# A graph network in fp32 on one core: the product h by seven half-size products with partial sums read from the banks, and first loads in blocks on two queues

## The chip, the cores and the metric

The kernel runs on one core of a Trainium2 chip. The metric is the device time of one execution in microseconds (us). Executions of one kernel mostly agree within 0.3%, so a difference of a few us is judged by several runs of both kernels in turn on the same chip.

PE is TensorE's matmul, PEld its weight load, DVE VectorE, ACT ScalarE, POOL GpSimd, SP SyncE; SPq, ACTq and POOLq are those engines issuing transfers.

## The reference

There are 4096 nodes with 512 features, all in fp32.

```python
# layer 0
bw = sign(w0); ba = max(sign(x), 0)
x = layernorm(x + relu(adj @ (ba @ bw.T)))
# layer 1
node_att = softmax(x @ node_w, axis=0)
h = x @ edge_w                                  # 4096 x 512: the change makes this cheaper
e = where(adj > 0, h @ h.T, -9e15)              # 4096 x 4096 scores
combined = node_att * softmax(e, axis=1)
x = layernorm(x + (adj * combined) @ (x @ w1) + bias)
```

## The kernel before

Four stages fill the time: x@w of layer 0 (bf16 signs), the aggregation over adj, h, and the scores h @ h.T in pairs of 512x512 blocks. The last stage, the weighted sum, runs on seven half-size products already (`lop` and `q` below), as did the preparation of its left operands.

```python
# start: one load for each of w0 and x^T, signed whole
w0 = stream.tile([P, KD, D], F32, name="w0", tag="stream")
nc.sync.dma_start(w0, w0_t.rearrange("(k p) o -> p k o", p=P))
# ... neg and bw on VectorE; nw_b, bias_b and we_s (1 MB) loaded by GpSimd
for g in range(NG):                                   # 8 groups of 512 rows
    xt = stream.tile([P, KD, W], F32, name="xt", tag="stream")
    nc.sync.dma_start(xt, x_t[:, ts(g, W)].rearrange("(k p) n -> p k n", p=P))
    ba = sp.tile([P, KD, W], BF16, name="ba", tag="hi")
    nc.vector.tensor_scalar(ba, xt, 0.0, None, ALU.is_gt)
    for j in range(BG):
        pw = ps_mm.tile([P, D], F32, name="pw", tag="mm")
        for k in range(KD):
            nc.tensor.matmul(pw, ba[:, k, ts(j, P)], bw[:, k, :], start=(k == 0), stop=(k == KD - 1))
        nc.scalar.copy(xw[:, g * BG + j, :], pw)

def aggregate(b):                                     # one of 32 row blocks of adj @ xw
    xb = rows.tile([P, D], F32, name="xb", tag="rows")
    nc.gpsimd.dma_start(xb, x[ts(b, P), :])           # 256 KB, on the GpSimd queue
    # ... 64 matmuls into acc, layernorm into xb, node_s and x1_d from it

for g in range(NG):                                   # h, transposed, over x1T in place
    ph = []
    for m in range(KD):
        p = ps_mm.tile([P, W], F32, name="ph", tag="mm")
        for k in range(KD):
            nc.tensor.matmul(p, we_s[:, k, ts(m, P)], x1T[:, k, ts(g, W)], start=(k == 0), stop=(k == KD - 1))
        ph.append(p)
    # ... copies of ph into x1T on ScalarE and VectorE
hT = x1T

blk = ctx.enter_context(tc.tile_pool(name="blk", bufs=11))    # takes the place that xw had
lopp = ctx.enter_context(tc.tile_pool(name="lopp", bufs=4))
adjp = ctx.enter_context(tc.tile_pool(name="adjp", bufs=2))

class Scores:                                          # one pair (A, B) of 512-row groups
    def load(self):                                    # 1 MB of adj for each direction
        a = blk.tile([P, BG, W], F32, name="a", tag="blk")
        nc.sync.dma_start(a, adj[ts(r, W), ts(c, W)].rearrange("(b p) w -> p b w", p=P))
    # prepare: one VectorE op on each a; main: scores pe, ScalarE's copy s, stats of them on VectorE;
    # turn: PE transposes s into pt; end: s and its transpose are stored to HBM

class Aggregate:                                       # the weighted sum, after all scores
    def load(self):
        a = adjp.tile([P, BG, BG, P], F32, name="ac")  # 1 MB of adj^T
        nc.gpsimd.dma_start(a, adj_t[ts(c, BG), :, ts(r, BG), :].rearrange("b p c i -> p b c i"))
    def main(self, between):
        lop = lopp.tile([P, BG, HD], F32, name="lop")  # 0.5 MB
        nc.sync.dma_start(lop, lop_d[self.r][:, m])
```

The point to keep in mind: the first two `ac` and four `lop` loads have free buffers, so they are issued as soon as h allows, although nothing uses them until about 1137 us. They share the transfer engines with the `a` blocks that the scores need at once.

Of the kernel before, what the change touches and what calls it, by code (L numbers as in the profile page):

```python
# [11 lines left out]
F32 = mybir.dt.float32  # L12
BF16 = mybir.dt.bfloat16
F32R = mybir.dt.float32r
AF = mybir.ActivationFunctionType
ALU = mybir.AluOpType
AX = mybir.AxisListType

P = 128
EPS = 1e-5  # L20
NEG_BIG = -9000000000000000.0
HUGE = 3.4e38


@with_exitstack
def kernel(
# [13 lines left out]
    nc = tc.nc  # L40
    N, D = x.shape
    NB = N // P
# [29 lines left out]
    lop_d = [dram.tile([P, 7, BG, HD], F32, name=f"lop_d{g}") for g in range(HG)]  # L72


    x1T = big.tile([P, KD, N], F32, name="x1T", tag="feat_major")

    def layernorm(ts_):
        n = len(ts_)
# [11 lines left out]
    with (  # L90
        tc.tile_pool(name="wide", bufs=1) as wide,
        tc.tile_pool(name="stream", bufs=3) as stream,
        tc.tile_pool(name="weights", bufs=1) as wp,
        tc.tile_pool(name="signs", bufs=2) as sp,
    ):

        xw = wide.tile([P, NB, D], F32R, name="xw", tag="node_major")
        nw_b = wp.tile([P, D], F32, name="nw_b")
        nc.gpsimd.dma_start(nw_b, bass.AP(tensor=node_w.tensor, offset=node_w.offset, ap=[[0, P], [1, D]]))

        bias_b = wp.tile([P, D], F32, name="bias_b")
        nc.gpsimd.dma_start(bias_b, bass.AP(tensor=bias.tensor, offset=bias.offset, ap=[[0, P], [1, D]]))


        w0 = stream.tile([P, KD, D], F32, name="w0", tag="stream")
        nc.sync.dma_start(w0, w0_t.rearrange("(k p) o -> p k o", p=P))
        neg = sp.tile([P, KD, D], BF16, name="neg", tag="hi")
        nc.vector.tensor_scalar(neg, w0, 0.0, None, ALU.is_lt)
        bw = wp.tile([P, KD, D], BF16, name="bw")
        nc.vector.scalar_tensor_tensor(bw, w0, 0.0, neg, ALU.is_gt, ALU.subtract)  # L110

        we_s = wp.tile([P, KD, D], F32, name="we_s")
        nc.gpsimd.dma_start(we_s, edge_w.rearrange("(k p) o -> p k o", p=P))

        for g in range(NG):
            xt = stream.tile([P, KD, W], F32, name="xt", tag="stream")
            nc.sync.dma_start(xt, x_t[:, ts(g, W)].rearrange("(k p) n -> p k n", p=P))
            ba = sp.tile([P, KD, W], BF16, name="ba", tag="hi")
            nc.vector.tensor_scalar(ba, xt, 0.0, None, ALU.is_gt)
            for j in range(BG):  # L120
                pw = ps_mm.tile([P, D], F32, name="pw", tag="mm")
                for k in range(KD):
                    nc.tensor.matmul(pw, ba[:, k, ts(j, P)], bw[:, k, :], start=(k == 0), stop=(k == KD - 1))  # L123
                nc.scalar.copy(xw[:, g * BG + j, :], pw)


        def aggregate(b):
            xb = rows.tile([P, D], F32, name="xb", tag="rows")
            nc.gpsimd.dma_start(xb, x[ts(b, P), :])
            acc = ps_mm.tile([P, D], F32, name="acc", tag="mm")  # L130
            for half in range(2):
                at = stream.tile([P, HB, P], F32, name="at", tag="stream")
                nc.sync.dma_start(at, adj_t[b, :, ts(half, HB), :])

                for q in range(2):
                    aq = at[:, ts(q, QC), :]
                    hi = sp.tile([P, QC, P], F32R, name="hi", tag="hi")
                    nc.scalar.copy(hi, aq)  # L138
                    lo = sp.tile([P, QC, P], F32R, name="lo", tag="lo")
                    nc.vector.tensor_sub(lo, aq, hi.bitcast(F32))  # L140
                    for c in range(QC):
                        kb = half * HB + q * QC + c
                        nc.tensor.matmul(acc, hi[:, c, :], xw[:, kb, :], start=(kb == 0), stop=False)  # L143
                        nc.tensor.matmul(acc, lo[:, c, :], xw[:, kb, :], start=False, stop=(kb == NB - 1))  # L144
            nc.vector.scalar_tensor_tensor(xb, acc, 0.0, xb, ALU.max, ALU.add)
            layernorm([xb])
            scr = wp.tile([P, D], F32, name="scr")
            nc.vector.tensor_tensor_reduce(
                scr, xb, nw_b, 1.0, 0.0, ALU.mult, ALU.add, accum_out=node_s[:, b : b + 1]
            )  # L150
            nc.gpsimd.tensor_add(scr, xb, bias_b)
            nc.gpsimd.dma_start(x1_d[ts(b, P), :], scr)
            return xb

        def left(b, low, high):

            to = lop_d[b // BG][:, :, b % BG, :]
            l11, l21, l12, l22 = low[:, :HD], low[:, HD:], high[:, :HD], high[:, HD:]
            sums_l = wp.tile([P, 4, HD], F32, name="sums_l", bufs=2)
            s4, s1, s2, s3 = (sums_l[:, n, :] for n in range(4))  # L160
            nc.gpsimd.tensor_sub(s3, l11, l21)
            nc.gpsimd.tensor_add(s1, l22, l21)
            nc.gpsimd.tensor_sub(s2, s1, l11)
            nc.gpsimd.tensor_sub(s4, l12, s2)
            nc.gpsimd.dma_start(to[:, 0, :], l11)
            nc.gpsimd.dma_start(to[:, 1:4:2, :], high.rearrange("p (h f) -> p h f", h=2))
            nc.gpsimd.dma_start(to[:, 2, :], s4)
            nc.gpsimd.dma_start(to[:, 4:, :], sums_l[:, 1:, :])

        def transpose_rows(b, xb):  # L170
            pt = ps_tr.tile([P, KD, P], F32, name="pt", tag="tr")
            for k in range(KD):
                nc.tensor.transpose(pt[:, k, :], xb[:, ts(k, P)], ident)  # L173
            nc.scalar.copy(x1T[:, :, ts(b, P)], pt)

        before = None
        for n in range(NB):
            b = n // 2 + n % 2 * HB
            xb = aggregate(b)
            if n % 2:  # L180
                left(n // 2, before[1], xb)
            if before is not None:
                transpose_rows(*before)
            before = (b, xb)
        transpose_rows(*before)


        for g in range(NG):
            ph = []
            for m in range(KD):  # L190
                p = ps_mm.tile([P, W], F32, name="ph", tag="mm")
                for k in range(KD):
                    nc.tensor.matmul(p, we_s[:, k, ts(m, P)], x1T[:, k, ts(g, W)], start=(k == 0), stop=(k == KD - 1))  # L193
                ph.append(p)
            for m in range(KD):
                if m % 2:
                    nc.vector.tensor_copy(x1T[:, m, ts(g, W)], ph[m])
                else:
                    nc.scalar.copy(x1T[:, m, ts(g, W)], ph[m])
    hT = x1T  # L200


    nmax = const.tile([P, 1], F32, name="nmax")
# [281 lines left out]
        some(1)  # L485


    over = big.tile([P, KD * N], F32, name="over", tag="feat_major")
    sums = over[:, : 2 * 7 * 2 * W].rearrange("p (g m h w) -> p g m h w", g=2, m=7, h=2)
    w1_s = over[:, 2 * 7 * 2 * W :].rearrange("p (k o) -> p k o", o=D)  # L490
    nc.sync.dma_start(w1_s, w1.rearrange("(k p) o -> p k o", p=P))
# [66 lines left out]
```

## Time and profile before

| | us |
|---|---|
| median of the timed runs | 2053.45 (2051.93 to 2053.71) |
| span of the profiled run | 2048.1 |
| idle time of PE | 35 |
| of which at the start | 16.4 |
| of which just after h | 4.8 |

The lines that carry this stand in the prediction. A timeline line gives the start, the duration, the engine, the line of the kernel, the operation with output and input, the number of records, and in brackets the idle time before it with what ended it. A row of the stage table gives the stretch, then busy time (and instructions) of PE, PEld, DVE, ACT and POOL, then the granted clock, the share of the transfer engines that was busy, and GB/s. What stands ahead of the `a` blocks in the queues after h is not shown there, so here it is, from the timeline of the kernel before:

```profile
636.33 1.30 SPq L393 DMA_DIRECT2D lop<-lop_d  x3
...
636.56 1.71 POOL L343 DMA_DIRECT2D ac<-in_adj_t_dram  x2 [90.33 <-PE ph L193]
...
639.10 2.06 SPq L393 DMA_DIRECT2D lop<-lop_d  x1
```

Two MB of `lop` and two of `ac` are issued within 5 us of h's end at 636.10, most of them ahead of the sixth `a` block.

### The profile page before, as it was taken

The numbers are of one execution on the slowest core, as the hardware profiler recorded it, in microseconds if no ns is written. First come the engines' busy times: TensorE is split into PE (matmuls) and PEld (weight loads), VectorE is DVE, ScalarE is ACT, GpSimd is POOL, SyncE is SP. The second block draws the span as 40 slices with busy tenths as digits, with TensorE's granted clock in tenths as the row PEclk, the third lists the DMA queues.
The fourth block names the chain that finished last, engine by engine and source line by source line (L and its number), as shares of the span: only waits on it lengthen the run. The fifth ranks groups of instructions, "written<-read, shape, count | busy, mean of one in ns | idle before, by whom it ended". The sixth has DMA issues, their size and how long they took to land.

```text
span 2048.1 us, 17627 instructions
## 1 busy us (share of the span) xinstructions
PE 2013.1 (98%) x6288; PEld 1113.3 (54%) x6288; DVE 1213.0 (59%) x1713; ACT 692.3 (34%) x1195; POOL 407.3 (20%) x512
## 2 busy tenths in 40 slices
PE   6999999999999999999999999999999999999997
PEld 3888888888544455555455544444444444444443
DVE  3555555555312454445445898687759775977634
ACT  4333333333102666666666631121211310221100
POOL 0334343343200000000001111240114111321101
PEclk9999999999999999999999999999999999999999
DMA  8565665565304777768776987576757765675421
GB/s 303 192 206 199 211 216 194 199 218 180 131 0 185 259 277 256 279 223 307 259 254 240 356 312 278 202 274 228 265 200 272 258 243 194 249 262 204 174 78 61
DMA packets 115623, 455.71 MB, mean 223 GB/s; under 512 B 10192, under 2 KB 10192, under 8 KB 90960
## 3 DMA queue, kind: packets, MB, share of 16 engines
q0 software_dynamic: 51120, 251.16, 32.7%
q1 hardware_dynamic: 64416, 203.44, 30.0%
q8 instruction: 49, 0.80, 0.2%
q14 instruction: 38, 0.31, 0.0%
HBM read 355.99 MB, written 98.57 MB: 222 GB/s over the span
## 4 chain that ended last, share of the span: by engine, by line
PE 97%; DMA 2%; DVE 1%; issue 0%; ACT 0%; SPq 0%; POOLq 0%; POOL 0%; DVEq 0%
PE ps L397 38%; PE pe L274 21%; PE acc L144 11%; PE acc L143 11%; PE ph L193 5%; PE po L449 5%; PE pt L295 3%; PE pw L123 1%; DMA xt<-in_x_t_dram 1%; DMA a<-in_adj_dram 1%; PE pt L173 1%; PE ptm L323 0%; DMA xb<-x_d 0%; DVE lo L140 0%; DMA out_dram<-xb 0%
## 5 line engine op out<-in xcount | busy, mean ns | idle before, releaser
L274 PE MATMUL pe<-x1T 128*128 128x512 f32 (+3 forms) x1152 | 477.3, 558 | 0.0
L397 PE MATMUL ps<-q,lop 128*128 128x512 f32 x1024 | 446.9, 592 | 0.0
L143 PE MATMUL acc<-xw,hi 128*128 128x512 f32 x1024 | 401.6, 392 | 0.0
L144 PE MATMUL acc<-xw,lo 128*128 128x512 f32 x1024 | 399.2, 390 | 0.5 <-DVE lo L140 0.5
L397 PE MATMUL ps<-t,lop 128*128 128x512 f32 x768 | 332.9, 592 | 0.0
L397 PEld LDWEIGHTS ps<-q,lop 128*128 128x128 f32 x1024 | 193.9, 190 | 240.8 <-issue 237.2
L274 PEld LDWEIGHTS pe<-x1T 128*128 128x128 f32 x1152 | 205.7, 191 | 184.8 <-issue 175.9
L352 ACT ACTIVATE q<-q 128x2048 f32<-128x2048 f32 x64 | 122.3, 1911 | 412.3 <-DVE q L349 400.9
L140 DVE TENSOR_TENSOR lo<-at,hi 128x1024 fp32r<-128x1024 f32 x128 | 166.6, 1302 | 147.0 <-ACT hi L138 146.9
L397 PEld LDWEIGHTS ps<-t,lop 128*128 128x128 f32 x768 | 145.9, 190 | 183.7 <-issue 178.9
L138 ACT CAST hi<-at 128x1024 fp32r<-128x1024 f32 x128 | 134.6, 1051 | 272.5 <-PE acc L143 268.3
L358 DVE SCALAR_TENSOR_TENSOR q<-ac,q 128x512 f32<-128x512 f32 x256 | 195.2, 815 | 51.5 <-ACT q L352 37.6
L144 PEld LDWEIGHTS acc<-xw,lo 128*128 128x128 f32 x1024 | 192.3, 188 | 40.3 <-DVE lo L140 0.9
L143 PEld LDWEIGHTS acc<-xw,hi 128*128 128x128 f32 x1024 | 192.3, 188 | 39.3
L256 DVE CUSTOM_DVE_ANT_0 a<-a,pe 128x512 f32<-128x512 f32 x112 | 76.9, 687 | 215.1 <-ACT s L281 215.1
L260 ACT ACTIVATE a<-a,nmax_c 128x512 f32<-128x512 f32 x256 | 183.4, 718 | 47.8 <-DVE nmax_c L256 47.3
L349 DVE CUSTOM_DVE_ANT_1 q<-q,mrow 128x2048 f32<-128x2048 f32 x64 | 152.4, 2387 | 47.3 <-DMA q<-s_d 39.2
L401 DVE TENSOR_TENSOR over<-over,ps 128x512 f32<-128x512 f32 x168 | 113.6, 681 | 103.3 <-PE ps L397 103.2
L343 POOL DMA_DIRECT2D ac<-in_adj_t_dram x64 | 49.0, 765 | 387.7 <-DVE q L358 280.1
L281 ACT COPY s<-pe 128x512 f32<-128x512 f32 (+2 forms) x144 | 78.0, 544 | 138.4 <-PE pe L274 117.2
L449 PE MATMUL po<-over 128*128 128x512 f32 x256 | 114.2, 592 | 3.8 <-DVE xb L458 3.8
L193 PE MATMUL ph<-x1T,we_s 128*128 128x512 f32 x256 | 110.2, 592 | 0.0
(88 smaller groups left out, 1491.7 us busy)
## 6 DMA issues: line engine op xcount, KB each, us to landing
at<-in_adj_t_dram SPq DMA_DIRECT2D x64, 1024.0 KB, 5.0
a<-in_adj_dram SPq DMA_DIRECT2D x64, 1024.0 KB, 7.8
ac<-in_adj_t_dram POOLq DMA_DIRECT2D x64, 1024.0 KB, 6.9
q<-s_d POOLq DMA_DIRECT2D x64, 1024.0 KB, 8.1
lop<-lop_d SPq DMA_DIRECT2D x112, 512.0 KB, 4.3
s_d<-s POOLq DMA_DIRECT2D x36, 1024.0 KB, 4.8
s_d<-t POOLq DMA_DIRECT2D x28, 1024.0 KB, 7.0
xt<-in_x_t_dram SPq DMA_DIRECT2D x8, 1024.0 KB, 8.2
```

Source lines behind the costliest of these rows:

```text
L138: nc.scalar.copy(hi, aq)
L140: nc.vector.tensor_sub(lo, aq, hi.bitcast(F32))
L143: nc.tensor.matmul(acc, hi[:, c, :], xw[:, kb, :], start=(kb == 0), stop=False)
L144: nc.tensor.matmul(acc, lo[:, c, :], xw[:, kb, :], start=False, stop=(kb == NB - 1))
L193: nc.tensor.matmul(p, we_s[:, k, ts(m, P)], x1T[:, k, ts(g, W)], start=(k == 0), stop=(k == KD - 1))
L260: lambda: nc.scalar.activation(e, e, AF.Exp, bias=nmax_c[:, b, c : c + 1], scale=-1.0, accum_out=sum_c[:, b, c : c + 1])
L274: nc.tensor.matmul(pe[:, lo * P :], hT[:, k, ts(A * BG + i, P)], hT[:, k, (B * BG + lo) * P : (B + 1) * W], start=(k == 0), stop=(k == KD ...
L349: nc.vector._custom_dve(TENSOR_ADD_SAT, out=q, in0=q, in1=mrow.unsqueeze(1).to_broadcast([P, BG, W]), s0=0.0, s1=-HUGE)
L352: nc.scalar.activation(q, q, AF.Exp)
L358: nc.vector.scalar_tensor_tensor(qc, a[:, :, c, :], 0.0, qc, ALU.max, ALU.mult)
L397: nc.tensor.matmul(ps, lop[:, c, ts(h, P)], rop[m][:, c, :], start=(c == 0), stop=(c == BG - 1))
L449: nc.tensor.matmul(po, (lower if k // 2 else upper)[:, k % 2, ts(i, P)], w1_s[:, k, :], start=(k == 0), stop=(k == KD - 1),)
```

## The change

Its intent: h by seven products of half size in place of eight, which saves an eighth of its matmuls. Partial sums stay in the banks, are read there in mid-group, and are added onto. This needs x1T and the result hT in different places, so xw and x1T exchange theirs. The start brings w0 and the first x^T in four blocks each, from two queues, signs them by blocks, and runs 12 matmuls on zeros to warm the clock. `xb`, `bias`, `node_w` and `edge_w` (1 MB, now loaded during the aggregation) move to the SP queue.

```diff
-    x1T = big.tile([P, KD, N], F32, name="x1T", tag="feat_major")
+    xw = big.tile([P, NB, D], F32R, name="xw", tag="large")
+    def seven(lop, rop, dests, after):
+        banks = [[ps_mm.tile([P, W], F32, name="seven", tag="mm") for q in range(2)] for _ in range(3)]
+        def multiply(bank, m, first, then):
+            for q in range(2):
+                for k in range(K):
+                    nc.tensor.matmul(banks[bank][q], lop(m, q)[k], rop(m)[k],
+                        start=(first and k == 0), stop=(k == K - 1), skip_group_check=not first)
+                then(banks[bank][q], q, *dests[q])
...
+        multiply(0, 0, True, m1)
+        multiply(1, 5, True, u2)
+        multiply(2, 4, True, nothing)
+        multiply(1, 6, False, u3)
+        multiply(0, 1, False, m2)
+        multiply(1, 3, False, m4)
+        multiply(2, 2, False, m3)
...
+            if g == 0:
+                for k in range(KD):
+                    nc.sync.dma_start(w0[:, k, :], w0_t[ts(k, P), :])
+                    nc.scalar.dma_start(xt[:, k, :], x_t[ts(k, P), ts(g, W)])
+                for _ in range(WARM):
+                    nc.tensor.matmul(pws[0], warm[:, :P], warm, start=True, stop=True)
+                # signs by blocks of 128x512 on VectorE
...
-            nc.gpsimd.dma_start(xb, x[ts(b, P), :])
+            nc.sync.dma_start(xb, x[ts(b, P), :])
...
+        hT = big.tile([P, KD, N], F32, name="hT", tag="large")
+        for g in range(HG):
+            # t1..t4 from x1T: three subtractions on VectorE, one on GpSimd
+            seven(...)
```

More of the change, by code (lines that the diff above doesn't have):

```diff
@@ L22 @@
 HUGE = 3.4e38
+WARM = 12
 @with_exitstack
@@ L72, with m1, u2, nothing @@
     lop_d = [dram.tile([P, 7, BG, HD], F32, name=f"lop_d{g}") for g in range(HG)]
-    x1T = big.tile([P, KD, N], F32, name="x1T", tag="feat_major")
+    xw = big.tile([P, NB, D], F32R, name="xw", tag="large")
+    def seven(lop, rop, dests, after):
+        K = len(rop(0))
+        banks = [[ps_mm.tile([P, W], F32, name="seven", tag="mm") for q in range(2)] for _ in range(3)]
+        def multiply(bank, m, first, then):
+            for q in range(2):
+                for k in range(K):
+                    nc.tensor.matmul(
+                        banks[bank][q],
+                        lop(m, q)[k],
+                        rop(m)[k],
+                        start=(first and k == 0),
+                        stop=(k == K - 1),
+                        skip_group_check=not first,
+                    )
+                then(banks[bank][q], q, *dests[q])
+                after(None, None)
+        def m1(ps, q, c11, c12, c21, c22):
+            nc.scalar.copy(c21, ps)
+        def u2(ps, q, c11, c12, c21, c22):
+            nc.vector.tensor_add(c12, c21, ps)
+        def nothing(*_):
+            pass
+        def u3(ps, q, c11, c12, c21, c22):
+            nc.vector.tensor_add(c22, c21, ps)
+            nc.vector.tensor_add(c22, c22, banks[2][q])
+            after(q, 3)
+        def m2(ps, q, c11, c12, c21, c22):
+            nc.scalar.copy(c11, ps)
+            after(q, 0)
+        def m4(ps, q, c11, c12, c21, c22):
+            nc.vector.tensor_add(c21, c21, ps)
+            after(q, 2)
+        def m3(ps, q, c11, c12, c21, c22):
+            nc.vector.tensor_add(c12, c12, ps)
+            after(q, 1)
+        multiply(0, 0, True, m1)
[5 more added lines that the diff above has]
+        multiply(2, 2, False, m3)
     def layernorm(ts_):
@@ L95 @@
     ):
-        xw = wide.tile([P, NB, D], F32R, name="xw", tag="node_major")
-        nw_b = wp.tile([P, D], F32, name="nw_b")
-        nc.gpsimd.dma_start(nw_b, bass.AP(tensor=node_w.tensor, offset=node_w.offset, ap=[[0, P], [1, D]]))
-        bias_b = wp.tile([P, D], F32, name="bias_b")
-        nc.gpsimd.dma_start(bias_b, bass.AP(tensor=bias.tensor, offset=bias.offset, ap=[[0, P], [1, D]]))
+        x1T = wide.tile([P, KD, N], F32, name="x1T")
+        warm = wp.tile([P, W], BF16, name="warm")
@@ L105 @@
+        nc.vector.memset(warm, 0.0)
         w0 = stream.tile([P, KD, D], F32, name="w0", tag="stream")
-        nc.sync.dma_start(w0, w0_t.rearrange("(k p) o -> p k o", p=P))
-        neg = sp.tile([P, KD, D], BF16, name="neg", tag="hi")
-        nc.vector.tensor_scalar(neg, w0, 0.0, None, ALU.is_lt)
         bw = wp.tile([P, KD, D], BF16, name="bw")
-        nc.vector.scalar_tensor_tensor(bw, w0, 0.0, neg, ALU.is_gt, ALU.subtract)
-        we_s = wp.tile([P, KD, D], F32, name="we_s")
-        nc.gpsimd.dma_start(we_s, edge_w.rearrange("(k p) o -> p k o", p=P))
@@ L115 @@
         for g in range(NG):
             xt = stream.tile([P, KD, W], F32, name="xt", tag="stream")
-            nc.sync.dma_start(xt, x_t[:, ts(g, W)].rearrange("(k p) n -> p k n", p=P))
             ba = sp.tile([P, KD, W], BF16, name="ba", tag="hi")
-            nc.vector.tensor_scalar(ba, xt, 0.0, None, ALU.is_gt)
-            for j in range(BG):
-                pw = ps_mm.tile([P, D], F32, name="pw", tag="mm")
+            pws = [ps_mm.tile([P, D], F32, name="pw", tag="mm") for j in range(BG)]
@@ L122 @@
+            if g == 0:
+                neg = sp.tile([P, KD, D], BF16, name="neg", tag="lo")
                 for k in range(KD):
-                    nc.tensor.matmul(pw, ba[:, k, ts(j, P)], bw[:, k, :], start=(k == 0), stop=(k == KD - 1))
-                nc.scalar.copy(xw[:, g * BG + j, :], pw)
+                    nc.sync.dma_start(w0[:, k, :], w0_t[ts(k, P), :])
[3 more added lines that the diff above has]
+                for k in range(KD):
+                    nc.vector.tensor_scalar(neg[:, k, :], w0[:, k, :], 0.0, None, ALU.is_lt)
+                    nc.vector.tensor_scalar(ba[:, k, :], xt[:, k, :], 0.0, None, ALU.is_gt)
+                    nc.vector.scalar_tensor_tensor(bw[:, k, :], w0[:, k, :], 0.0, neg[:, k, :], ALU.is_gt, ALU.subtract)
+                order = [(k, j) for k in range(KD) for j in range(BG)]
+            else:
+                nc.sync.dma_start(xt, x_t[:, ts(g, W)].rearrange("(k p) n -> p k n", p=P))
+                nc.vector.tensor_scalar(ba, xt, 0.0, None, ALU.is_gt)
+                order = [(k, j) for j in range(BG) for k in range(KD)]
@@ new lines @@
+            for k, j in order:
+                nc.tensor.matmul(pws[j], ba[:, k, ts(j, P)], bw[:, k, :], start=(k == 0), stop=(k == KD - 1))
+                if k == KD - 1:
+                    nc.scalar.copy(xw[:, g * BG + j, :], pws[j])
+        nw_b = wp.tile([P, D], F32, name="nw_b")
+        nc.sync.dma_start(nw_b, bass.AP(tensor=node_w.tensor, offset=node_w.offset, ap=[[0, P], [1, D]]))
+        bias_b = wp.tile([P, D], F32, name="bias_b")
+        nc.sync.dma_start(bias_b, bass.AP(tensor=bias.tensor, offset=bias.offset, ap=[[0, P], [1, D]]))
@@ L127, in aggregate @@
+        we_s = wp.tile([P, KD, D], F32, name="we_s")
         def aggregate(b):
             xb = rows.tile([P, D], F32, name="xb", tag="rows")
-            nc.gpsimd.dma_start(xb, x[ts(b, P), :])
+            nc.sync.dma_start(xb, x[ts(b, P), :])
             acc = ps_mm.tile([P, D], F32, name="acc", tag="mm")
@@ L179 @@
             xb = aggregate(b)
+            if n == 1:
+                nc.sync.dma_start(we_s, edge_w.rearrange("(k p) o -> p k o", p=P))
             if n % 2:
@@ L185 @@
         transpose_rows(*before)
-        for g in range(NG):
-            ph = []
-            for m in range(KD):
-                p = ps_mm.tile([P, W], F32, name="ph", tag="mm")
-                for k in range(KD):
-                    nc.tensor.matmul(p, we_s[:, k, ts(m, P)], x1T[:, k, ts(g, W)], start=(k == 0), stop=(k == KD - 1))
-                ph.append(p)
-            for m in range(KD):
-                if m % 2:
-                    nc.vector.tensor_copy(x1T[:, m, ts(g, W)], ph[m])
-                else:
-                    nc.scalar.copy(x1T[:, m, ts(g, W)], ph[m])
-    hT = x1T
+        hT = big.tile([P, KD, N], F32, name="hT", tag="large")
+        HK = KD // 2
+        lops = stream.tile([P, 4, HK, HD], F32, name="lops", tag="stream")
+        l11, l12 = we_s[:, :HK, :HD], we_s[:, HK:, :HD]
+        l21, l22 = we_s[:, :HK, HD:], we_s[:, HK:, HD:]
+        s4, s1, s2, s3 = (lops[:, n] for n in range(4))
+        nc.gpsimd.tensor_add(s1, l21, l22)
+        nc.gpsimd.tensor_sub(s2, s1, l11)
+        nc.gpsimd.tensor_sub(s3, l11, l21)
+        nc.gpsimd.tensor_sub(s4, l12, s2)
+        left_h = l11, l12, s4, l22, s1, s2, s3
+        for g in range(HG):
+            r11, r12 = (x1T[:, :HK, ts(c, W)] for c in (g, g + HG))
+            r21, r22 = (x1T[:, HK:, ts(c, W)] for c in (g, g + HG))
+            t1, t2 = (sp.tile([P, HK, W], F32, name="t12", tag="hi") for _ in range(2))
+            t3, t4 = (sp.tile([P, HK, W], F32, name="t34", tag="lo") for _ in range(2))
+            nc.vector.tensor_sub(t1, r12, r11)
+            nc.gpsimd.tensor_sub(t3, r22, r12)
+            nc.vector.tensor_sub(t2, r22, t1)
+            nc.vector.tensor_sub(t4, r21, t2)
+            right_h = r11, r21, r22, t4, t1, t2, t3
+            seven(
+                lambda m, q: [left_h[m][:, k, ts(q, P)] for k in range(HK)],
+                lambda m: [right_h[m][:, k, :] for k in range(HK)],
+                [[hT[:, q + f, ts(c, W)] for f in (0, HK) for c in (g, g + HG)] for q in range(2)],
+                lambda *_: None,
+            )
     nmax = const.tile([P, 1], F32, name="nmax")
@@ L485 @@
         some(1)
-    over = big.tile([P, KD * N], F32, name="over", tag="feat_major")
+    over = big.tile([P, KD * N], F32, name="over", tag="large")
     sums = over[:, : 2 * 7 * 2 * W].rearrange("p (g m h w) -> p g m h w", g=2, m=7, h=2)
```

## The prediction

> **What bounds the kernel now.** I read the page first, then one table by stage (busy time of each engine in stretches that I cut where the kernel's phases meet), then PE's own waits, then the timelines at the places those waits name. From the page:
>
> ```profile
> span 2048.1 us, 17627 instructions
> PE 2013.1 (98%) x6288; PEld 1113.3 (54%) x6288; DVE 1213.0 (59%) x1713; ACT 692.3 (34%) x1195; POOL 407.3 (20%) x512
> ...
> L193 PE MATMUL ph<-x1T,we_s 128*128 128x512 f32 x256 | 110.2, 592 | 0.0
> ```
>
> PE is busy for 98%, so time is won in two ways only: fewer matmuls, or fewer of PE's 35 us of idleness. The last row is all of h: 128 matmuls in fp32, each shown as two records, so 110.2/128 = 0.861 us each (the mean of 592 ns counts overlapped pipeline time). The stages (us, PE busy, PEld, DVE, ACT, POOL busy, clock, DMA share, GB/s):
>
> ```profile
> 0.00:45.86 45.86, 29.51 (x129) 13.08 (x130) 14.62 (x12) 20.18 (x33) 4.79 (x13) 1.00 0.93 332
> 45.86:525.24 479.38, 478.90 (x2168) 395.87 (x2168) 266.83 (x344) 158.99 (x190) 180.78 (x212) 1.00 0.58 195
> 525.24:636.10 110.86, 110.86 (x266) 49.40 (x265) 20.73 (x31) 12.52 (x22) 8.70 (x10) 1.00 0.16 57
> 636.10:1152.20 516.10, 511.33 (x1652) 263.36 (x1651) 255.27 (x610) 330.09 (x783) 40.76 (x74) 1.00 0.75 268
> ```
>
> Row 1 is layer 0's x@w, row 2 its aggregation, row 3 h, row 4 the scores. Rows 2 and 3 have no gaps, so h costs what its matmuls cost. PE's own waits:
>
> ```profile
> PE pw L123 <- DVE ba L119: 16.4, 2, 16.0
> PE pt L295 <- ACT s L281: 4.8, 1, 4.8
> PE po L449 <- DVE xb L458: 3.8, 1, 3.8
> ```
>
> The first is the start, the second lies just after h, the third at the end, which the change doesn't touch. The start and the place after h in the timeline (start, duration):
>
> ```profile
> 16.02 5.16 PE L123 MATMUL pw<-bw,ba 128*128 128x512 bf16 x16 [16.02 <-DVE ba L119]
> ...
> 525.43 4.49 SPq L245 DMA_DIRECT2D a<-in_adj_dram  x5
> ...
> 544.28 0.38 POOL L206 PARTITION_ALL_REDUCE gmax<-nmax  x1 [8.48 <-issue]
> ...
> 653.98 1.23 DVE L250 TENSOR_SCALAR a<-a 128x2048 f32<-128x2048 f32 x1 [7.96 <-DMA a<-in_adj_dram]
> ...
> 657.19 0.91 PE L295 MATMUL pt<-ident,s 128*128 128x128 f32 x4 [4.77 <-ACT s L281]
> 657.89 5.08 PE L274 MATMUL pe<-x1T 128*128 128x512 f32 x8
> ```
>
> The first 1 MB of x^T lands only at 14.7 us, because 2.6 MB from the GpSimd queue share the first 16 us with it. After h, the sixth score block of adj lands at 653.95, VectorE waits for it in order, ScalarE's copies wait for VectorE, and PE idles 4.77 us; then eight records take 5.08 us where later ones take 3.60, another 1.5. This place costs 6.2 us now.
>
> **What the Trainium skill says.** "TensorE: Matmul & The Clock Gate", Part 1: the array's clock starts at half rate and falls back to it after some 3.4 us of idleness. The trace agrees: the first 16 bf16 matmuls took 5.16 us, the later 112 ran at 24.35/112 = 0.217 us (16 = 3.48). "PSUM — Partial Sum Buffer", The four PSUM rules: a matmul without the first flag adds onto what the bank holds, and a synchronised read in mid-group is allowed. The change rests on this; no run shows it yet. "DMA: Bandwidth & Descriptors", Issuing engines are not separate DMA queues: two issuing queues save issue time only. The trace moves 380 to 410 GB/s whenever much is queued, from one queue (397 at 534 to 537 us) as from two. "SBUF — State Buffer", Who interferes with whom: a two-input VectorE operation contends with GpSimd's reads. The 128x512 GpSimd add took 1.27 us with VectorE mostly idle and 2.20 beside `lo`.
>
> **The change part by part.**
> 1. *h.* Products 128 -> 4 groups x 7 products x 2 halves x 2 = 112 matmuls: 16 x 0.861 = 13.8 us less, all of it on the path. Added beside PE, for each group of 24.1 us: VectorE 3 subtractions of 128x1024 at about 1.25 and 10 additions of 128x512 at 0.69 = 10.7 us; ScalarE 4 copies at 0.58; GpSimd one 128x1024 subtraction at about 2.9 (the joins' mean). All fit. The order of instructions in the changed build shows no partial-sum bank reused sooner than one product (3.44 us) after the two to three VectorE operations that read it. One new wait: on VectorE, two of the first group's subtractions (1.25 each) come ahead of the last row block's layernorm. Counted from the last aggregation matmul, that block was ready after 528.2 - 525.24 = 3.0; now 5.5. PE has 0.45 transposes + 3.44 + 0.86 = 4.75 of work before it: it idles about 0.8. Net 13.8 - 0.8 = 13.0; h lasts about 98.
> 2. *Start.* GpSimd's loads go; w0 and the first x^T come as 8 blocks of 256 KB. The trace's ramp (1.24 MB by 6.0 us) puts the four pairs at about 4.5, 5.8, 7.3 and 8.6 us. VectorE then needs per pair 0.43 + 0.43 + 0.69 = 1.5 us (from 1.23 and 2.29 at four times the width), so it ends near 10.5, and group 0 near 11.4. The second x^T is the third MB of the queue: 3.1 MB at 0.39 MB/us after about 3 us, so landed by 11.5, signed by 12.8. From there seven groups x 3.48 = 24.4: the stage ends at 37.2, not 45.86. The 12 warm-up matmuls lie under the loads and save the 1.7 us of cold clock (counted in this). Gain 8.6; I take 8.3, since the third x^T waits for the last signs and may leave a small gap.
> 3. *After h.* xw and x1T change places. Before, xw's place was free at 525, so five score blocks were loaded under h (row of 525.43). Now that place holds x1T until h's last product, and the build shows the first load of adj waiting for exactly that matmul. The 4.8 us wait thus doesn't vanish with h: it gets another cause. In the queue ahead stand 1.57 MB of lop and, sharing, 2.1 MB of ac, both issued one product earlier (data from about -1.5 us after h). The fourth block of a, which VectorE must prepare before three of the four diagonal rows' statistics, lands after (1.57 + 2.1 + 4.2)/0.40 - 1.5 = 18.2 us, up to 20.5 if the 16 engines run apart as before. Then preparation 1.23, three statistics 2.3, exponential and copy 1.5: the transposes are ready at 23.2 to 25.5. PE's own work till there is 21.3. So PE idles about 2 to 4, 3.5 with some cold clock, instead of 6.2: gain 2.7. Later statistics catch up by my walk through the order; the rest of the program has the same instructions in nearly the same order.
> 4. *xb, bias, node_w on SP.* A row block's load waits for a buffer that was free some 20 us before the block behind it is needed (one row block takes 15 us); hidden: 0.
>
> Sum: 13.0 + 8.3 + 2.7 = 24.0 us. 2053.45 - 24.0 = 2029.4.
>
> **The rivals.**
> (a) *The lost prefetch becomes the bound after h.* For: all nine blocks of a, lop and ac come at once, and DMA ran full for 18 us there even with five blocks already in. Against: my count of PE's 21.3 us of other work. If the fourth block lands at 26, PE idles 10 and the time is near 2036.
> (b) *GpSimd holds up h.* Changing between the partition reduction and ordinary arithmetic costs 8.5 us (row of 544.28; 8.6 once before the joins). The new order switches four times and has the second group's subtraction behind two of them: ready about 33.5 us after aggregation, needed at 36. Slack of 2.5 only; if reductions or contention take 5 us more, 2 to 3 us are lost and ScalarE's copies behind the softmax of node_att are late too: 2032.
> (c) *The first loads are bandwidth, not issue.* 3.1 MB still pass before group 1. If the ramp on two queues is no better and VectorE's chain starts a microsecond or two later, the start gains 6: 2031 to 2032. If the blocks land faster, 10: 2027.
> (d) *VectorE becomes h's bound.* 10.7 of 24.1 us speaks against; if true, h would stay near 110 and the time near 2042.
>
> **Range and chances.** (a) to (c) are worth -2 to +7 together, so 2023 to 2037. Faster by over 2% means below 2012.4, which needs 17 us that no part offers: 0.02. Slower by over 2% would need a stall of 65 us: 0.01. Within 2%: 0.97.
>
> **What would show it.** In the changed profile: 224 records of h in about 98 us; PE's first real matmul near 6 us and aggregation beginning at 37; a gap under 1 us a few us after aggregation; PE's wait for transposes `pt` some 21 us after h, of 2 to 4 us, with the chain of waits passing through loads of a; all a loads starting at h's end. Wrong would be: gaps inside h behind GpSimd, an idle stretch over 8 us after h, gaps between groups of x@w, or waits for xb in the aggregation.

## The result, and the profile after

The changed kernel is correct. Its median is 2027.82 us (2026.51 to 2029.48, 4 runs) against 2052.74 for the kernel before (4 runs): ratio 0.9879, 95% interval 0.9862 to 0.9896. A ratio is the mean time of one kernel's runs over that of the other's from the same rounds, so it is not quite the ratio of the medians. The verdict is "same" at the 2% mark, with 25 us gained where 24.0 were predicted.

The page of the changed kernel, and its table by stage:

```profile
span 2025.5 us, 17689 instructions
...
PE 2004.4 (99%) x6268; PEld 1108.3 (55%) x6268; DVE 1243.5 (61%) x1759; ACT 691.5 (34%) x1195; POOL 401.5 (20%) x485
```

```profile
0.00:12.90 12.90, 9.10 (x28) 3.23 (x29) 6.83 (x15) 3.22 (x5) 0.69 (x6) 1.00 0.87 297
12.90:37.90 25.00, 24.75 (x113) 10.99 (x113) 8.59 (x7) 16.87 (x30) 0.00 (x0) 1.00 1.02 392
...
517.40:614.90 97.50, 97.39 (x234) 43.45 (x233) 43.88 (x61) 12.41 (x22) 15.41 (x16) 1.00 0.05 17
614.90:1129.00 514.10, 509.65 (x1650) 262.22 (x1649) 260.33 (x613) 328.96 (x783) 39.40 (x72) 1.00 0.76 278
```

Behind the two rows of x@w and the aggregation, whose row is left out, comes h: 97.5 us, with PE busy for 97.39 of them, so nothing beside PE holds it up although VectorE's work there doubled from 20.73 to 43.88. In the last row, the scores, PE still misses 4.45 us. Its own waits say where:

```profile
PE pt L377 <- ACT s L363: 4.5, 2, 2.9
PE po L531 <- DVE xb L540: 3.7, 1, 3.7
PE pw L181 <- DVE ba L178: 1.6, 2, 1.3
```

The 16 us wait at the start is gone, and the one wait for transposes after h has become two. The timeline of the changed kernel at the start, at h's beginning and after h (which ends at 614.95):

```profile
12.90 3.63 PE L181 MATMUL pw<-bw,ba 128*128 128x512 bf16 x16 [1.33 <-DVE ba L178]
...
522.64 0.63 PE L238 MATMUL pt<-ident,xb 128*128 128x128 f32 x4
...
611.75 1.28 SPq L475 DMA_DIRECT2D lop<-lop_d  x3
...
612.29 1.71 POOL L425 DMA_DIRECT2D ac<-in_adj_t_dram  x2 [29.01 <-PE seven L89]
...
615.25 23.95 SPq L327 DMA_DIRECT2D a<-in_adj_dram  x9
...
639.33 1.14 PE L377 MATMUL pt<-ident,s 128*128 128x128 f32 x8 [2.91 <-ACT s L363]
...
656.01 1.23 DVE L332 TENSOR_SCALAR a<-a 128x2048 f32<-128x2048 f32 x1 [3.80 <-DMA a<-in_adj_dram]
...
659.22 0.66 PE L377 MATMUL pt<-ident,s 128*128 128x128 f32 x4 [1.54 <-ACT s L363]
```

The `a` loads now start at h's end, behind `lop` and `ac`, and PE, out of work 21.5 us after h, waits 2.91 us, until 24.4 us after h. The second stall, of 1.54 us, ends when the ninth `a` block, the last of the row of 615.25, has landed at 656.0 and been prepared. The chain of waits up to 640 us (view `--critical`: start, duration, what) shows when it was issued, and behind what:

```profile
636.58 2.23 ACT a L342 x6
...
638.83 17.15 DMA a<-in_adj_dram
```

Its buffer came free only when ScalarE's exponentials on an earlier block were done, and these had waited for the statistics behind the fourth block. It then took 17.15 us to land, while the transfer engines were fully busy.

To compare kernels I cut each profile at the first aggregation matmul, at the transposes after the last one, at the first score product, and at the first product of the weighted sum. The differences from the kernel before, in us:

| kernel | x@w | aggregation | h | scores | rest | span |
|---|---|---|---|---|---|---|
| before (us) | 45.51 | 479.73 | 110.86 | 515.97 | 896.03 | 2048.1 |
| changed | -8.20 | +0.59 | -13.54 | -1.75 | +0.30 | -22.6 |
| start | -8.66 | +0.32 | -0.01 | -3.60 | -1.35 | -13.3 |
| start_again | -8.53 | +0.31 | 0.00 | -3.47 | +1.59 | -10.1 |
| start_xb | -3.06 | -0.02 | 0.00 | -1.11 | +0.89 | -3.3 |
| h | -0.14 | +0.28 | -13.55 | -2.17 | +1.18 | -14.4 |
| swap | +0.70 | -0.72 | -0.02 | -0.51 | +1.85 | +1.3 |
| before_gate | -0.05 | -0.73 | -0.02 | -0.57 | +2.07 | +0.7 |
| after_gate | -8.34 | +0.60 | -13.55 | -0.79 | -1.32 | -23.4 |
| spread | -6.51 | +0.63 | -13.55 | -6.70 | +0.33 | -25.8 |
| nowarm | -8.35 | +0.59 | -13.55 | -2.86 | +0.17 | -24.0 |
| onequeue | -7.55 | -0.14 | -13.54 | -2.17 | +0.30 | -23.1 |
| whole | -2.49 | -0.59 | -13.55 | -1.66 | +1.49 | -16.8 |
| before_again | -0.03 | -0.04 | -0.01 | +0.62 | +2.66 | +3.2 |

Each profile is one execution. The runs are described below. The last row is the kernel before profiled again: it shows how far one profile may lie from another of the same kernel, mostly in "rest" and always by the clock, as the experiments will show. The table's sum for the change (22.6) is lower than the gain in the medians (24.9) because the first profile of the kernel before was a lucky one: by the second profile the sum would be 25.8.

### The profile page after: what moved, and what is told of

Same layout as the page of the kernel before. It is cut to its first block, busy times and chain, and to the rows that moved or that the text cites. A ratio compares the mean times of both kernels' runs of the same rounds, so it can differ in the third digit from the quotient of the medians. Undisturbed runs are those within 1.5% of the kernel's fastest.

```text
span 2025.5 us, 17689 instructions
## 1 busy us (share of the span) xinstructions
PE 2004.4 (99%) x6268; PEld 1108.3 (55%) x6268; DVE 1243.5 (61%) x1759; ACT 691.5 (34%) x1195; POOL 401.5 (20%) x485
## 4 chain that ended last, share of the span: by engine, by line
PE 96%; DMA 3%; DVE 1%; ACT 0%; issue 0%; SPq 0%; ACTq 0%; POOLq 0%; POOL 0%; DVEq 0%
PE ps L479 38%; PE pe L356 21%; PE acc L209 11%; PE acc L208 11%; PE po L531 5%; PE seven L89 5%; PE pt L377 3%; DMA a<-in_adj_dram 2%; PE pw L181 1%; PE pt L238 1%; DMA xt<-in_x_t_dram 1%; DVE lo L205 0%; PE ptm L405 0%; DMA xb<-x_d 0%; ACT a L342 0%
## 5 line engine op out<-in xcount | busy, mean ns | idle before, releaser
L356 PE MATMUL pe<-hT 128*128 128x512 f32 (+3 forms) x1152 | 475.5, 557 | 0.0
L356 PEld LDWEIGHTS pe<-hT 128*128 128x128 f32 x1152 | 205.0, 191 | 184.0 <-issue 174.8
L377 PEld LDWEIGHTS pt<-ident,s 128*128 128x128 f32 x496 | 62.1, 141 | 68.7 <-issue 57.7
```

The lines of the kernel that those rows point to most:

```text
L356: nc.tensor.matmul(pe[:, lo * P :], hT[:, k, ts(A * BG + i, P)], hT[:, k, (B * BG + lo) * P : (B + 1) * W], start=(k == 0), stop=(k == KD ...
L377: nc.tensor.transpose(pt[:, j, :], s[:, i, ts(j, P)], ident)
```

## The experiments

All were correct, and were timed in five rounds against the kernel before.

**start and h: each half alone.** The first puts only the new start (blocks, signs, warm-up, `xb` and the small loads on SP) into the kernel before; the second puts only the seven products and the exchanged places there.

```diff
 # start: the kernel before with
+  the blocks, the signs, WARM, nw_b, bias_b, we_s and xb loads of the changed kernel
 # h: the changed kernel with
-  that start
+  the start of the kernel before
```

> The kernel before with the new start alone (first loads in blocks on two queues, signs on VectorE, xb and the two small loads moved), its 128 matmuls for h untouched. Theory A, the parts add: the aggregation begins at about 37.3 us instead of 45.9, h keeps 110.9 us, the 6.2 us after h stay, and the time falls by 7.6 us, to about 2045. Theory B, the start's gain is partly given back later (aggregation waits for adjacency blocks that now come too late, or the moved xb load delays h): the aggregation takes over 1 us longer and the time falls by less than 5.

> The changed kernel with the old start (one load each for x and w on the GpSimd queue, signs as before); h by seven products. Theory A, the parts add: x@w ends at about 45.9 us, h takes 97.3 us, what is lost after h falls by 1.75, and the time falls by 15.3 us, to about 2037.5. Theory B, part of the gain in h needs the new start (xb's earlier load): h takes over 99 us and the time falls by under 14.

start: median 2039.42, ratio 0.9936 (0.9924 to 0.9949), so about 13.1 us gained. h: 2035.10, ratio 0.9918 (0.9904 to 0.9931), about 16.8 gained. Together they would give 29.9; the change gives 24.8 by its ratio. The intervals of the three gains are about 3 us either way, so the missing 5.1 us is only about as large as its own uncertainty. Each expectation was right for its own stage (-8.66 and -13.55). For the time, h's 15.3 lies within its interval and start's 7.6 below its own, since start also shortens the stretch after h. (The expectation of h puts the first x and w on the GpSimd queue; they are on SP there, as in the kernel before.) Timelines of start and of h after h:

```profile
630.54 0.59 SPq L404 DMA_DIRECT2D lop<-lop_d  x1
...
646.35 0.66 PE L306 MATMUL pt<-ident,s 128*128 128x128 f32 x4 [2.28 <-ACT s L292]
```

```profile
646.78 1.93 PE L367 MATMUL pt<-ident,s 128*128 128x128 f32 x8 [2.61 <-ACT s L353]
648.50 2.77 PE L346 MATMUL pe<-hT 128*128 128x512 f32 x4
```

The wait of 4.77 us is 2.28 in start (and 0.38 at the next transposes) and 2.61 in h, but 2.91 and 1.54 in the changed kernel. So the scores are 3.60 and 2.17 us shorter in start and in h, and only 1.75 in the change: in these profiles that is 4.0 of what is missing. Why the two halves together do not shorten the wait is not shown. Part of it can be scatter: changed, nowarm, onequeue and whole have the same instructions after h and wait there 4.45, 3.34, 2.54 and 3.19 us in all.

**start_again and before_again: is that chance?** Both are second profiles of kernels that ran already.

```diff
 (no edit)
```

> The same kernel as start, a second profile, since it gained 13 us where its stage of x@w gained 8.3. Theory A, the extra 5 us are real and lie after h: the wait for transposes is again 2 to 3 us and not 4.8, without slow matmuls behind it, and the ratio is again near 0.9936. Theory B, they are chance (when the queues' bytes land, and whether the idle time tips the clock): the wait or the slow stretch comes out differently this time, between 2 and 6.5 us in all, and the ratio moves by 0.001 to 0.002.

> The kernel before against itself, with a second profile: ratio 1.000. Theory A, what is lost after h is a property of the order of its loads: again 4.8 us of wait and 1.5 us of slow matmuls, and the matmuls at the end (po) again 7.1 us. Theory B, it is chance in part: the wait is anywhere from 2 to 5 us, the slow stretches come and go by 1.5 to 1.8 us at each of the places where PE idles over 2 us.

start_again: median 2039.72, ratio 0.9935. before_again: median 2052.37, ratio 0.9998 (0.9985 to 1.0011). The wait after h in before_again, and PE's last products in it:

```profile
657.03 1.11 PE L295 MATMUL pt<-ident,s 128*128 128x128 f32 x4 [4.69 <-ACT s L281]
657.94 5.57 PE L274 MATMUL pe<-x1T 128*128 128x512 f32 x8
...
2031.84 9.92 PE L449 MATMUL po<-over 128*128 128x512 f32 x16 [3.70 <-DVE xb L458]
```

and those last products in the first profile of the kernel before:

```profile
2031.36 7.13 PE L449 MATMUL po<-over 128*128 128x512 f32 x16 [3.77 <-DVE xb L458]
```

Two things separate here. The length of the wait came out nearly the same in the second profile: 4.77 and 4.69 in the kernel before, 2.28 and 2.40 in start. What follows a wait is chance: the same 16 records behind the same idle time took 7.13 us once and 9.92 the next time, because the clock was at half speed for a while. In start the same `po` records took 7.13 and 9.68 us. Over the profiles of the change and its variants with an idle of 2.5 to 2.9 us after h, the clock fell in three (h 2.61, onequeue 2.54, whole 2.57) and held in two (changed 2.91, nowarm 2.64). Each fall cost 1.4 to 1.7 us (in onequeue the granted clock was 0.50 for 3.4 us). So theory A of start_again held for the wait, and theory B of before_again for the slow stretches.

**start_xb: which part of the start shortens the wait?**

```diff
-            nc.sync.dma_start(xb, x[ts(b, P), :])
+            nc.gpsimd.dma_start(xb, x[ts(b, P), :])
```

> The kernel start with the loads of xb back on the GpSimd queue; everything else of the new start stays. Theory A, moving xb to the other queue is what made the fourth lop load after h issue in 0.59 us instead of 2.06 and the wait for transposes shrink from 4.7 to 2.4 us in start: here the issue takes 2 us again, the wait is 4.5 us or more, and the time is 2042 or more (ratio 0.9950 or more). Theory B, it is another part of the new start: the wait stays at 2 to 3 us and the time at 2038 to 2040.5. In both, the aggregation begins up to 2 us later than at 36.9 if the xb loads share the first microseconds with the blocks, and within 0.3 us of it if they don't.

Median 2046.85, ratio 0.9970 (0.9956 to 0.9984): 7 us of the 13 are lost by this one line. From the timeline of start_xb:

```profile
15.54 24.66 PE L125 MATMUL pw<-bw,ba 128*128 128x512 bf16 x100 [1.91 <-DVE ba L122]
...
653.10 1.11 PE L306 MATMUL pt<-ident,s 128*128 128x128 f32 x4 [3.76 <-ACT s L292]
```

The aggregation begins at 42.45 us in place of 36.85, which is more than the 2 us that both theories allowed. On the GpSimd queue four `xb` loads of 256 KB are issued at 1.3 to 4.2 us, where no buffer holds them back, and they pass among the first blocks: the last two block groups come at 10.08 and 12.61 us and the second group at 15.54, where start had 8.83, 10.11 and 12.77. PE idles between them, the clock falls (it was granted 0.73 from 10 to 20 us), and 2.8 of the 5.6 us are that: from the second group's start to the aggregation it takes 26.91 us here and 24.08 in start. On the SP queue `xb` lines up behind the blocks. After h neither theory fits: the fourth `lop` load was issued in 0.59 us as in start, not in 2.06 as in the kernel before (2.16 in its second profile), and the wait is 3.76 us, between the two. Why that load's issue takes 2 us in one kernel and 0.6 in another, in the same place of the same order of loads, stays open, and so does what makes up the 2.4 us by which the kernel before waits longer than start.

**swap: the lost head start.** The changed kernel gave up loading `a` under h. This run does the same to the kernel before, and keeps its 128 matmuls.

```diff
-    x1T = big.tile([P, KD, N], F32, name="x1T", tag="feat_major")
+    xw = big.tile([P, NB, D], F32R, name="xw", tag="large")
+    hT = big.tile([P, KD, N], F32, name="hT", tag="large")   # after xw's end; h is written there
```

> The kernel before with the places of two buffers exchanged, so that the adjacency loads for the scores can no more start during h than in the changed kernel; h still by 128 matmuls of 0.861 us. Theory A, the wait after h comes from the bytes that are queued ahead of the a blocks and not from a lost head start: h stays 110.9 us, the wait after h is 3 to 6 us, and the time is within 2 us of the kernel before. Theory B, the lost head start costs: the wait after h grows to over 8 us, and the time rises by 3 us or more.

Median 2051.22, ratio 0.9996 (0.9983 to 1.0008). From its timeline:

```profile
636.29 23.47 SPq L245 DMA_DIRECT2D a<-in_adj_dram  x9
...
655.67 0.33 PE L295 MATMUL pt<-ident,s 128*128 128x128 f32 x1 [4.25 <-ACT s L296]
```

No `a` load comes before h's end at 636.06, and the wait is 4.25 us where it was 4.77. Theory A's numbers held: without the head start of five blocks the kernel is no slower. The wait ends here with the third block, which landed 16.5 us after h, and in the kernel before with the sixth, 17.9 us after. But this build also puts its nine `a` loads ahead of `lop`, unlike the changed kernel. What that order gains and what the head start was worth could cancel, and no run separates them.

**before_gate and after_gate: hold back what nobody needs yet.** A one-element copy ties the first use of six buffers to a result of the tenth pair of score blocks.

```diff
                 a = adjp.tile([P, BG, BG, P], F32, name="ac")
+                if self.g == 0 and self.r == 0 and len(self.a) < 2:
+                    nc.vector.tensor_copy(a[:, 0, 0, 0:1], nmax_c[:, BG, 3:4])
...
                 lop = lopp.tile([P, BG, HD], F32, name="lop")
+                if self.g == 0 and self.r == 0 and m in (0, 1, 2, 4):
+                    nc.vector.tensor_copy(lop[:, 0, 0:1], nmax_c[:, BG, 3:4])
```

> The kernel before with its first two ac loads and first four lop loads held back behind the a blocks. Theory A, those bytes ahead of the a blocks made the 6.2 us lost after h (4.77 of idle, 1.5 of slow matmuls behind it): the wait falls under 1 us and the time by about 6, to 2046.5. Theory B, the wait is for the a blocks' own bytes and their preparation: the wait falls by less than 2 us and the time by less than 2.5.

> The changed kernel with the first two ac loads and the first four lop loads held back behind the a blocks that the transposes need first. Theory A, the bytes of ac and lop ahead of the a blocks make both stalls after h (2.91 and 1.54 us): both vanish, the scores stage falls by 4 to 4.5 us and the time to about 2023.4. Theory B, the a blocks' own bytes and the later wait for a buffer make the second stall: the first shrinks by up to 3 us, the second stays at 1.5 or grows, and the time falls by 1 to 3. Theory C, what is held back is missed later (the products wait for lop or ac): a new wait of some us takes the place of the old, and the time stays within 1 us.

before_gate: median 2050.80, ratio 0.9995. after_gate: 2026.57, ratio 0.9876. The stalls after h are gone from both profiles, and others stand 150 us later. From the timeline of after_gate:

```profile
780.78 0.66 PE L377 MATMUL pt<-ident,s 128*128 128x128 f32 x4 [0.78 <-ACT s L363]
...
787.86 0.66 PE L377 MATMUL pt<-ident,s 128*128 128x128 f32 x4 [2.98 <-ACT s L363]
788.35 5.29 PE L356 MATMUL pe<-hT 128*128 128x512 f32 x8
```

The six loads, 4 MB, were all released at 764.5 us and pushed the `a` blocks of that moment aside: 3.76 us of stall and 1.7 of slow clock in place of 4.45. So theory A had the cause right (those bytes make the stalls) and its gain wrong; the outcome is the one named as theory C, though what was missed was not the held-back loads but the next `a` blocks. before_gate paid the same: its wait after h is gone, as its theory A said, but it stalls for 1.00 and 3.05 us later, and its time is only theory B's.

**spread: hold each back to a different pair.**

```diff
+                    A, B = ((1, 3), (1, 5))[len(self.a)]
+                    nc.vector.tensor_copy(a[:, 0, 0, 0:1], nmax_c[:, A * BG, B : B + 1])
...
+                    A, B = {0: (1, 7), 1: (2, 4), 2: (2, 6), 4: (3, 5)}[m]
+                    nc.vector.tensor_copy(lop[:, 0, 0:1], nmax_c[:, A * BG, B : B + 1])
```

> The changed kernel with its first two ac and first four lop loads each held back behind a different pair of score blocks, some 30 us apart, instead of all six at once as in after_gate. Theory A, the stalls are made by bytes that come together and nothing that is held back is needed before 1114 us: no wait of PE for transposes is left in the scores, and the 4.5 us of the changed kernel's two stalls are gained: a span of 2021 to 2022 where the tail's clock is as in the changed kernel, a time of about 2022.5 to 2024. Theory B, any load of 0.5 to 1 MB that joins the a blocks costs a stall of its own: several stalls of 0.3 to 3 us, and the time stays at 2026 to 2028.

Median 2021.78 (2021.37 to 2024.11), ratio 0.9850 (0.9836 to 0.9864) against 0.9879 for the change: about 6 us better than the changed kernel, and the fastest of all. The two longest of PE's waits in spread (the end and the start; the rest are shorter and at the start too), and the stretch after h first in spread, then in the changed kernel:

```profile
PE po L537 <- DVE xb L546: 3.6, 1, 3.6
PE pw L181 <- DVE ba L178: 2.4, 1, 2.4
```

```profile
616.00:670.00 54.00, 54.00 (x173) 27.80 (x173) 28.59 (x59) 30.59 (x74) 3.23 (x5) 1.00 0.92 335
```

```profile
615.00:669.00 54.00, 49.55 (x159) 25.30 (x158) 27.65 (x56) 27.04 (x67) 3.05 (x5) 1.00 1.00 378
```

No wait for transposes is left anywhere. The transfer engines go from fully busy at 378 GB/s to 0.92 at 335, and PE is busy for all 54 us. Theory A held, with a time somewhat under its 2022.5 to 2024. (In this profile the second group of x@w began 0.7 us later than in the changed kernel, and the groups behind it lost 1.0 us more to the clock; the timed runs are the measure.)

**nowarm, onequeue, whole: the parts of the start,** each in the changed kernel.

```diff
 # nowarm
-                for _ in range(WARM):
-                    nc.tensor.matmul(pws[0], warm[:, :P], warm, start=True, stop=True)
 # onequeue
-                    nc.scalar.dma_start(xt[:, k, :], x_t[ts(k, P), ts(g, W)])
+                    nc.sync.dma_start(xt[:, k, :], x_t[ts(k, P), ts(g, W)])
 # whole: w0 and xt by one 1 MB load each, still on two queues, and signed by one operation each
```

> The changed kernel without its 12 warm-up matmuls on zeros. Theory A, they only fill time in which TensorE waits for data and buy a warm clock: the first groups of x@w run at 0.43 us a matmul instead of 0.22, which is 16 matmuls of 0.21 more, some of it hidden in the waits for blocks: x@w ends 0.5 to 2 us later, and so does the kernel. Theory B, the data set the pace of the start: the second x block is signed at 11.6 us whatever TensorE did, x@w ends at 37.3 us as before and the time stays within 0.5 us.

> The changed kernel with the x blocks issued by the same engine as the w blocks, one queue instead of two. Theory A, two queues save no more than issue time, since both feed the same transfer engines: [...]the blocks land in the order of issue, and x@w ends within 0.5 us of 37.3. Theory B, one queue carries less than two: the first blocks land 2 us or more later and x@w ends at 39 us or more.

> The changed kernel with the first x and the first w loaded whole, 1 MB each, and signed whole by VectorE, still on two queues. Theory A, the blocks are what gains: the first matmul of x@w waits for 2 MB and a sign of the whole, so it begins at about 13.4 us instead of 6.2, x@w ends at about 41.3 and the time rises by about 4 us. Theory B, the order of bytes is the same and TensorE catches up behind the second x block: x@w ends within 1 us of 37.3 and the time rises by less than 1.

nowarm: median 2025.86, ratio 0.9872, as fast as the change (0.9879) within the intervals. onequeue: 2028.44, ratio 0.9885; the aggregation begins at 37.96, 0.65 later, a little outside what theory A allowed. whole: 2031.08, ratio 0.9899, 3 to 4 us slower than the change; the aggregation begins at 43.02, 5.7 later, in a profile that was the slowest of its four runs. From the timelines of nowarm and of whole:

```profile
5.99 5.61 PE L179 MATMUL pw<-bw,ba 128*128 128x512 bf16 x16 [5.99 <-DVE bw L172]
12.90 1.47 PE L179 MATMUL pw<-bw,ba 128*128 128x512 bf16 x6 [1.30 <-DVE ba L176]
```

```profile
12.92 30.45 PE L179 MATMUL pw<-bw,ba 128*128 128x512 bf16 x128 [7.25 <-DVE bw L172]
```

Without warm-up most of the first 16 matmuls run at the slow clock (until 9.8 us their weight loads follow each other by 0.43 us) and end at 11.60, and the second group begins at 12.90, the same moment as in the changed kernel, since it waits for the second x^T. The warm-up buys nothing here (theory B). In whole the first product waits until 12.92, as expected, and the 7.25 us of idleness undo the warm-up: 30.45/128 is 0.238 us a matmul, 2.9 us more than at 0.215, which is why the stage ends at 43.0 and not at 41.3. So the blocks are worth 3 to 4 us of time, the second queue about 0.6, the warm-up nothing, and keeping `xb` out of the first microseconds about 5.6 up to the aggregation. Each was taken away alone, so these do not sum to the gain, and no run puts `edge_w`, `bias` and `node_w` back on the GpSimd queue.

## Why the prediction was right

**h: 13.0 predicted, 13.54 measured** (13.55 in the run without the new start). The count of matmuls, 16 x 0.861 = 13.8, is the whole of it. The 0.8 us of idleness behind the last layernorm was too much: PE's previous record ends at 522.52 and the transposes of the last row block start at 522.64, a gap of 0.1. I had put both subtractions ahead of that layernorm; VectorE took the block's relu and sum at 518.75, before t4 at 519.35. Rivals (b) and (d) fell: GpSimd's reductions held up nothing (it idled 5.63 us ahead of the first, not 8.5), the second t3 was ready 26.4 us after the aggregation and not 33.5, and VectorE was busy for 43.88 of 97.5 us. All runs with the seven products were correct, so the rule on banks that the prediction took from the Trainium skill is borne out: they were read in mid-group and then added onto.

**Start: 8.3 predicted, 8.20 measured, of which 0.59 went back** in the aggregation (0.3 in start and h too; no run isolates it). The size was right and the list of causes was not. The warm-up was said to save 1.7 us and saves nothing. Part 4 gave the moved `xb` a 0, looking only at whether its load is hidden; start_xb shows that its place in the first microseconds is worth 5.6 us. The sum was right because part 2 had counted that GpSimd's loads go. Rival (c) in its simple form fell too: the second x^T was signed at 12.9 us, as worked out. A second queue that was worth 0.65 us agrees with what the prediction took from the skill on issuing engines. Its own reading for that was wrong in two points: from 534 to 537 us GpSimd's stores ran beside the `a` loads, and from 6 to 16 us the kernel before moved only 339 GB/s with the transfer engines busy throughout (share 1.00). SP's x^T loads alone moved 390 (14 to 22 us of the changed kernel).

**After h: 2.7 predicted, 1.75 measured in this profile.** The first stall came in kind, place and size as worked out: the fourth `a` block landed 19.8 us after h (18.2 to 20.5 predicted), and PE waited until 24.4 us after h, for 2.91 us (2 to 4). The step that failed is "Later statistics catch up": a second stall of 1.54 us followed (0.70 in nowarm, 0.62 in whole, none in onequeue). I walked the order of the statistics but not the ninth `a` block: its buffer comes free only behind the late fourth block, and it then took 17.15 us to land (17.58 in whole; in nowarm the second stall comes 55 us after h, behind a block whose buffer a store held).
Rival (a) fell by the changed profile itself: its fourth block landed at 19.8 us and not at 26, and PE idled 4.45 us and not 10. The waits after h in both kernels had the cause that I gave to the one in the changed kernel, the bytes queued ahead: before_gate and after_gate take both away by holding back `lop` and `ac`.

**The sum** of 24.0 against 24.9 by the medians is therefore partly luck: half a us too little for h, 0.7 too much for the start with its wait, 1 too much after h; and the clock, which is not in the sum, moves single executions by 1.4 to 2.8 us at each place where PE idles and it falls.

## What to carry to other kernels

A wait at the head of a stage can be made by transfers that are issued early only because their buffers are free; give each a reason to start later, and a different one for each, or the burst only moves. Two changes that each shorten the same wait need not shorten it further together, so measure the parts alone before adding them. Ask of a load that is "hidden" what it passes on its way: 1 MB among the first blocks delayed the next stage by 5.6 us here, about as much as loading in blocks had brought it forward.

## What the Trainium skill lacked or had wrong

- "TensorE: Matmul & The Clock Gate", Part 1, has the clock fall after at least one idle window of about 3.4 us. Here idle times of 2.54, 2.57 and 2.61 us were followed by matmuls at half speed, and others of 2.64 and 2.91 us were not. The free-running window that the page describes fits such chance; the length that suffices was shorter here, and each fall cost 1.4 to 1.7 us.
- No page says when matmuls on zeros are worth issuing to warm the array in a kernel. Where the data set the pace, as in nowarm, 12 warm-up matmuls changed the median by 2 us in the wrong direction (2027.82 with, 2025.86 without; the intervals overlap).
- "GPSIMD Engine Reference", 2.1 Instruction dispatch, gives about 6 us for the first call to freshly loaded code. Ahead of the first partition reduction, in the middle of the kernel, GpSimd idled 8.41 to 9.29 us in six profiles (8.48 in the kernel before, 9.01 in before_gate), with nothing else shown that it waits for, and 5.63 to 5.78 us in the eight others; the page does not say that a reduction between ordinary arithmetic pays such a price. That it is this load of code is my reading, and no run tests it.
- No page tells why the issue of one 0.5 MB load took 2.06 and 2.16 us in the two profiles of the kernel before and 0.59 us in start, start_again and start_xb, in the same place of the order.
